# The last half's rows brought in and normalised one half earlier, its neighbour's scalings on GpSimd, and the exactness check moved from half 11 to half 1

## The chip, the cores and the metric

The kernel runs on one core of a Trainium2 chip. The metric is the device time of one execution in microseconds (us). Three runs of the kernel before took 2614.74, 2616.55 and 2617.44 us; the median is 2616.55 us.

## The reference: what is computed

`x` has 3327 rows of 512 numbers, `adj` is a 3327 x 3327 matrix of zeros and ones (about 1% ones).

```python
def gat_layer(x, W, adj):                 # used twice, W of 512 x 1024
    Wh, Ws = split(x @ W, 2, axis=-1)
    a = softmax(Wh @ Ws.T, axis=-1) * adj
    return leaky_relu(a @ Wh + x, 0.01)

def sign_layer(x, adj, weight):           # weight of 512 x 512
    xw = maximum(sign(x), 0) @ sign(weight).T
    return relu(adj @ xw)

x = layernorm(x + gat_layer(gat_layer(x, W[0], adj), W[1], adj))
x = layernorm(x + sign_layer(x, adj, weight))
```

The change concerns the very last part: `adj @ xw`, the relu, the sum with the layer-normed rows, and the last layernorm.

## The kernel before, in words

The 3327 rows are 26 tiles of 128 (the last has 127), two tiles make a half, so there are NQ = 13 halves, numbered 0 to 12. Two attention passes take most of the time: each goes through 13 x 13 steps of a half of output rows against a half of keys, with seven products instead of eight for each 2 x 2 block of tiles. The second pass also leaves behind what the last layer needs: `h_d` in DRAM holds the rows `h` ahead of the first layernorm, `mv` their means and variances, `adj_d` the seven block sums of the adjacency in 8 bits, and `xw` the product of signs in 16 bits. It also counts, in `cnt`, the adjacency entries that are neither 0 nor 1 (`exact`): 8 bits carry the block sums only of such a matrix.

`finale` is the last layer. For each half g it has 91 matmuls (`aggregate`, L1138): 13 pairs of tiles by seven products, which collect in four PSUM banks, b = 0 to 3. (In half 12 two of the products have other places and one a bank of its own.) Many matmuls of halves 0 and 1 are issued earlier, as filling between the last steps of attention; what half 1 has left are 14. Around the matmuls of a half, these are the steps:

- `load_h(g + 1)`: SyncE loads two tiles of `h_d` into `ho` (four buffers in all, so a tile waits until the tile four before it has been stored).
- `standard(t)` (L1166, L1167): two ScalarE instructions give a tile of `ho` the first layernorm.
- `take_out(g, b)` (L1179 to L1190): ScalarE copies the first product of bank 0 (L1179), VectorE adds the products together into `c`.
- `moments(t)` (L1195 to L1201): VectorE computes `ho = max(c, 0) + ho` (L1195) and its mean and variance (L1197, L1199), ScalarE the square root (L1201).
- `scaled(t)` (L1208, L1209): VectorE takes the reciprocal and scales the tile; then GpSimd issues the store to `out` (L115).
- `check`, once: VectorE reduces `cnt` to one number per partition (`bad`, L1213), TensorE transposes that (`pbad`, L1215), VectorE reduces it to one number and casts it (`flag`, `flag_i`, L1216, L1217).

After half 12's matmuls every engine loads `flag_i` into a register and branches (L1260, L1261). If the count is zero, the short tail is run: half 12 is taken out of PSUM piece by piece, each piece followed by its share of the moments (L1274, L1275, L1280), the second tile is scaled on ScalarE (L1303, L1304), the first on VectorE (L1209), and both are stored. Otherwise the layer is computed again from the adjacency in 32 bits.

No scheduler orders this work. Each half collects pairs of a place between 0 and 1 and a function in the list `work`; the matmuls stand at even distances, the other steps at the places written beside them. The list is sorted by place and run in that order, and each engine gets its instructions in the order in which they are written. An engine runs its own list strictly in order: if an instruction waits, all behind it wait.

Of the kernel before, what the change touches and what calls it, by code (L numbers as in the profile page):

```python
# [15 lines left out]
ALU = mybir.AluOpType  # L16
AX = mybir.AxisListType
# [13 lines left out]
def kernel(  # L31
# [8 lines left out]
    nc = tc.nc  # L40
# [6 lines left out]
    NQ = NT // 2  # L47
    assert NT % 2 == 0 and D == 4 * P

    def rows(t):  # L50
        return min(P, N - t * P)
# [7 lines left out]
    def half_tiles(g):  # L59

        return (2 * g, 2 * g + 1)
# [28 lines left out]
    cnt = keep.tile([P, NQ * NQ], F32, name="cnt")  # L90
# [19 lines left out]
    def load_rows(eng, dst, src, r):  # L110

        cut = r - r % 16
        engines = eng if isinstance(eng, tuple) else (eng,)
        if cut:
            engines[0].dma_start(out=dst[:cut], in_=src[:cut])  # L115
        if cut < r:
            engines[-1].dma_start(out=dst[cut:r], in_=src[cut:r])
# [437 lines left out]
    def attention(l, att):  # L555
# [514 lines left out]
        for e in fill:  # L1070
            aggregate(*e)
        finale(att)


# [42 lines left out]
    def load_aggregate(g, s):  # L1117
        n = min(JL, NQ - s * JL)
        t = slot([P, JL, 7, P], F8, f"ahl_{g}_{s}")
        nc.sync.dma_start(out=t[:, :n], in_=adj_d[g][:, s * JL : s * JL + n])  # L1120
        for p in range(n):
            ah[g, s * JL + p] = t[:, p]

    def aggregate(g, b, p, i):
        if p == 0 and (i == BANKS[b][0] or (g, i) == (NQ - 1, 5)):
            pool, tag = (ps_acc, "acc") if g % 2 else (ps_ch, "ch") if b < 3 else (ps_tr, "tr")
            if g == NQ - 1 and i == 5:

                (pool, tag), b = (ps_acc, "acc"), 4
            po[g, b] = pool.tile([P, 2, HD], F32, tag=tag, name=f"agg_{g}_{b}")  # L1130
        x1, x2, t = xw[2 * p], xw[2 * p + 1], xt.get(p)
        if i < 2:
            of = (x1, x2)[i][:, :HD]
        else:
            of = (t[:, 1], t[:, 2], t[:, 0], x2[:, HD:], t[:, 3])[i - 2]

        own = (g, i) == (NQ - 1, 5)
        nc.tensor.matmul(  # L1138
            po[g, 4 if own else b][:, i % 2], ah[g, p][:, BLOCKS[i]], of,
            start=(p == 0 and (own or i % 2 == 0)), stop=(p == NQ - 1), skip_group_check=True,  # L1140
        )

    def finale(att):
# [5 lines left out]
        bad = small.tile([P, 1], F32, tag="bad", bufs=1, name="bad")  # L1149
# [8 lines left out]
        def load_h(g):  # L1158
            for t in half_tiles(g):
                h = h_of[t] = att.tile([P, D], F32, tag="adj", bufs=4, name=f"ho_{t}")  # L1160
                load_rows(nc.sync, h, h_d[t * P : t * P + rows(t), :], rows(t))

        def standard(t):
            h = h_of[t][: rows(t)]
            r = rows(t)
            nc.scalar.activation(h, h, AF.Identity, bias=nmean[:r, t : t + 1])  # L1166
            nc.scalar.activation(h, h, AF.Identity, scale=rstd[:r, t : t + 1])  # L1167

        def take_out(g, b):
            def s(name):  # L1170
                tmp[name] = att.tile([P, HD], F32, tag=f"o{name}", bufs=1, name=f"a{name}_{g}")
                return tmp[name]

            if b == 0:
                c_of[g] = [ring.tile([P, D], F32, tag="h", name=f"c_{t}") for t in half_tiles(g)]
            lo, hi = c_of[g]
            k = po[g, b]
            if b == 0:
                nc.scalar.copy(s("p1"), k[:, 0])  # L1179
                nc.vector.tensor_tensor(lo[:, :HD], k[:, 1], tmp["p1"], ALU.add)  # L1180
            elif b == 1:
                nc.vector.tensor_tensor(s("u2"), k[:, 0], tmp["p1"], ALU.add)
                nc.vector.tensor_tensor(s("u3"), k[:, 1], tmp["u2"], ALU.add)
            elif b == 2:
                c12 = lo[:, HD:]
                nc.vector.tensor_tensor(c12, k[:, 0], tmp["u2"], ALU.add)
                nc.vector.tensor_tensor(c12, k[:, 1], c12, ALU.add)
                nc.vector.tensor_tensor(hi[:, HD:], k[:, 0], tmp["u3"], ALU.add)
            else:
                nc.vector.tensor_tensor(hi[:, :HD], k[:, 0], tmp["u3"], ALU.add)  # L1190

        def moments(t, c, tag=""):
            r = rows(t)
            h = h_of[t][:r]
            nc.vector.scalar_tensor_tensor(h, c[:r], 0.0, h, ALU.max, ALU.add)  # L1195
            st = small.tile([P, 6], F32, tag="bn", name=f"bo{tag}_{t}")
            nc.vector.bn_stats(st[:r], h)  # L1197
            m2 = small.tile([P, 2], F32, tag="mv2", name=f"mo{tag}_{t}")
            nc.vector.bn_aggr(m2[:r], st[:r])  # L1199
            rs = small.tile([P, 1], F32, tag="rs", name=f"rs{tag}_{t}")  # L1200
            nc.scalar.activation(rs[:r], m2[:r, 1:2], AF.Sqrt, bias=eps[:r])  # L1201
            out_of[t] = m2, rs

        def scaled(t, *engines):
            r = rows(t)
            h = h_of[t][:r]
            m2, rs = out_of[t]
            nc.vector.reciprocal(rs[:r], rs[:r])  # L1208
            nc.vector.tensor_scalar(h, h, m2[:r, 0:1], rs[:r], ALU.subtract, ALU.mult)  # L1209
            load_rows(engines, out[t * P : t * P + r, :], h, r)  # L1210

        def check():
            nc.vector.reduce_max(bad, cnt, axis=AX.X)  # L1213
            pb = ps_tr.tile([1, P], F32, tag="tr", name="pbad")
            nc.tensor.transpose(pb, bad, ident)  # L1215
            nc.vector.reduce_max(flag, pb, axis=AX.X)  # L1216
            nc.vector.tensor_copy(flag_i, flag)  # L1217
# [4 lines left out]
        for g in range(NQ):  # L1222
            todo = [
                (b, p, i) for b in range(4) for p in range(NQ) for i in BANKS[b]
                if g > 1 or (g, b) == (0, 3) or p >= EARLY
            ]
            if g == NQ - 1:

                todo = [e for e in todo if e[0] < 2] + [
                    (b, p, i) for b, i in ((3, 6), (2, 4), (2, 5)) for p in range(NQ)  # L1230
                ]
            work = [
                ((n + 0.5) / len(todo), lambda e=e: aggregate(g, *e))
                for n, e in enumerate(todo)
            ]
            done = {b: (n + 1) / len(todo) for n, (b, p, i) in enumerate(todo)}
            t1, t2 = half_tiles(g)
            if g + 3 < NQ:
                work += [
                    (s / NS, lambda s=s: load_aggregate(g + 3, s)) for s in range(NS)  # L1240
                ]
            if g + 1 < NQ:
                work.append((0.5, lambda: load_h(g + 1)))
            work += [(0.1, lambda: standard(t1)), (0.4, lambda: standard(t2))]
            if g == NQ - 2:
                work.append((0.95, check))
            if g < NQ - 1:
                for b in range(3):
                    work.append((done[b] + 0.02, lambda b=b: take_out(g, b)))
                work += [(0.98, lambda: moments(t1, c_of[g][0]))]  # L1250
            if g > 0:
                u1, u2 = half_tiles(g - 1)
                work += [
                    (0.05, lambda: take_out(g - 1, 3)), (0.08, lambda: scaled(u1, nc.gpsimd)),
                    (0.1, lambda: moments(u2, c_of[g - 1][1])),
                    (0.2, lambda: scaled(u2, nc.gpsimd)),
                ]
            for _, do in sorted(work, key=lambda e: e[0]):
                do()
        inexact = nc.values_load(flag_i[0:1, 0:1], min_val=0, max_val=2 * CW)  # L1260
        with tc.If(inexact < 1) as cmp:  # L1261

            t1, t2 = half_tiles(g0)
# [33 lines left out]
            r = rows(t2)  # L1297
            m2, rs = out_of[t2]
# [3 lines left out]
            h = h_of[t2][:r]  # L1302
# [4 lines left out]
            half(t1, hi)  # L1307
            both(t1)
            scaled(t1, nc.sync)
        with cmp.Else():  # L1310

            for t in range(NT):
                r = rows(t)
# [13 lines left out]
                h = h_of[t] = att.tile([P, D], F32, tag="adj", bufs=4, name=f"hf_{t}")  # L1327
# [44 lines left out]
```

## Time and profile before

The profiled execution took 2613.8 us, of which the span that the profile shows is 2612.0 us; the table gives places in that span. The profiled run is 2.75 us shorter than the median of the three timed runs.

| stage | us from the span's start | what stands there |
|---|---|---|
| filling matmuls, 16-bit, and the rest of half 0 and 1 | 2472 to 2491.8 | TensorE back to back |
| half 2 | 2491.84 to 2501.77 | 91 matmuls, 9.93 us; VectorE busy 9.17 us |
| half 10 | 2571.31 to 2581.24 | 91 matmuls, 9.93 us; VectorE busy 6.95 us |
| half 11 | 2581.24 to 2592.1 | 91 matmuls and the check |
| half 12's matmuls | 2592.1 to 2602.2 | the last work of TensorE |
| tail on VectorE and ScalarE | 2598.08 to 2606.76 | taking out, moments, scaling |
| last stores | 2605.56 to 2612.0 | |

In half 12 TensorE and VectorE work beside each other. GpSimd issues nothing but stores in this part of the kernel. TensorE is busy 99% of the span, VectorE 81%, GpSimd 42%, ScalarE 31%. Rows of the timeline give the start and the duration of an instruction or a merged group; in brackets stands how long its engine had been idle, and for whom it waited.

### The profile page before, as it was taken

Reading aid. Unit: us, or ns where it says so; the run is one execution under the profiler, and the core shown is the slowest. Engines: PE = TensorE matmul, PEld = TensorE weight load, DVE = VectorE, ACT = ScalarE, POOL = GpSimd, SP = SyncE. Lnnn points to the kernel's source line nnn. Section 1 sums busy time; section 2 is a strip of 40 time slices with the busy share of each in tenths; the row PEclk is TensorE's granted clock in tenths of the full one; section 3 lists DMA queues with packets and bytes.
Section 4 is the critical chain, followed back from the end, with each engine's and each line's share of the span. In section 5 each row is a group of like instructions: output and inputs, shape, how many; then the busy total and the mean of one; then the engine's idle time right before and its main releaser. Section 6 shows DMA issues by size and latency. Waiting matters only on the chain. (4 is left out here: it accounts for less than half of the span.)

```text
span 2612.0 us, 40098 instructions
## 1 busy us (share of the span) xinstructions
PE 2581.2 (99%) x12536; PEld 2235.2 (86%) x12536; DVE 2111.2 (81%) x4422; ACT 800.5 (31%) x1978; POOL 1095.4 (42%) x2026
## 2 busy tenths in 40 slices
PE   9999999999999999999999999999999999999998
PEld 7888888888888888887888888888888888888787
DVE  5754888899888996768874689989899898776976
ACT  3323332333333332221332333333333333222143
POOL 3640344444434444456662044434444444454611
PEclk9999999999999999999999999999999999999999
DMA  6855777777777877698865668777787777677775
GB/s 210 295 195 176 244 240 265 241 267 253 256 247 238 277 237 237 224 264 251 301 242 178 227 223 282 246 254 257 239 282 245 249 261 237 232 260 260 261 254 184
DMA packets 309784, 639.15 MB, mean 245 GB/s; under 512 B 35049, under 2 KB 177987, under 8 KB 308028
## 3 DMA queue, kind: packets, MB, share of 16 engines
q1 hardware_dynamic: 273868, 530.29, 62.4%
q0 software_dynamic: 35696, 106.21, 10.9%
q8 instruction: 103, 1.69, 0.3%
q14 instruction: 117, 0.96, 0.1%
HBM read 529.69 MB, written 106.67 MB: 244 GB/s over the span
## 5 line engine op out<-in xcount | busy, mean ns | idle before, releaser
L586 PE MATMUL pZ<-gs,xs 128*128 128x256 f32 x2496 | 636.9, 380 | 3.0 <-ACT u L603 2.9
L793 POOL TENSOR_TENSOR as<-s 128x128 f32<-128x128 f32 x338 | 163.2, 483 | 1051.2 <-DVE s L755 866.5
L586 PEld LDWEIGHTS pZ<-gs,xs 128*128 128x128 f32 x2496 | 473.0, 190 | 71.3 <-ACT u L603 6.4
L820 PE MATMUL acc<-ws,s 128*128 128x256 f32 x1352 | 402.4, 379 | 0.5 <-DVE h L855 0.5
L820 PE MATMUL acc<-wh,s 128*128 128x256 f32 x1352 | 355.7, 379 | 0.7 <-DVE s L755 0.4
L820 PE MATMUL acc<-ws,as 128*128 128x256 f32 x1352 | 348.0, 380 | 4.2 <-POOL as L795 4.1
L745 ACT ACTIVATE s<-s 128x512 f32<-128x512 f32 x338 | 213.3, 631 | 396.6 <-DVE s L739 395.6
L586 PE MATMUL pY<-gs,xs 128*128 128x256 f32 x1248 | 320.9, 380 | 4.4 <-ACT p L603 4.4
L820 PEld LDWEIGHTS acc<-ws,as 128*128 128x128 f32 x1352 | 256.0, 190 | 45.8 <-POOL as L795 8.6
L820 PEld LDWEIGHTS acc<-wh,s 128*128 128x128 f32 x1352 | 256.6, 190 | 36.7 <-DVE s L755 1.9
L820 PEld LDWEIGHTS acc<-ws,s 128*128 128x128 f32 x1352 | 255.7, 190 | 36.0 <-DVE h L855 1.7
L586 PEld LDWEIGHTS pY<-gs,xs 128*128 128x128 f32 x1248 | 236.5, 190 | 38.7 <-ACT p L603 6.7
L656 DVE TENSOR_TENSOR top<-top,s 128x512 f32<-128x512 f32 x286 | 200.7, 716 | 72.3 <-ACT s L643 52.8
L739 DVE TENSOR_TENSOR s<-s,off 128x512 f32<-128x512 f32 x338 | 246.4, 729 | 0.6
L755 DVE TENSOR_TENSOR s<-s,adj 128x512 f32<-128x512 f32 x338 | 239.1, 707 | 9.5 <-DMA adj<-in_adjT_dram 1.5
L750 DVE TENSOR_TENSOR total<-total,s 128x512 f32<-128x512 f32 x312 | 230.4, 738 | 0.0
L795 POOL TENSOR_TENSOR as<-s 128x128 f32<-128x128 f32 x338 | 202.6, 599 | 26.5
L603 ACT COPY u<-pZ 128x256 f32<-128x256 f32 x312 | 115.6, 371 | 306.9 <-PE pZ L586 303.8
L820 PE MATMUL acc<-wh,as 128*128 128x256 f32 x676 | 202.4, 381 | 0.0
L794 POOL TENSOR_TENSOR s<-s 128x128 f32<-128x128 f32 x338 | 184.4, 546 | 27.4
L796 POOL TENSOR_TENSOR as<-s,as 128x128 f32<-128x128 f32 x338 | 182.2, 539 | 26.5
L628 DVE TENSOR_TENSOR s<-p,u 128x256 f32<-128x256 f32 x156 | 67.0, 430 | 137.8 <-ACT u L603 136.7
(219 smaller groups left out, 3890.8 us busy)
## 6 DMA issues: line engine op xcount, KB each, us to landing
ws<-ws_d SPq DMA_DIRECT2D x338, 512.0 KB, 3.8
xs<-xs_d SPq DMA_DIRECT2D x182, 512.0 KB, 5.7
adj<-in_adjT_dram SPq DMA_DIRECT2D x324, 256.0 KB, 4.2
xs<-xs_d SPq DMA_DIRECT2D x156, 384.0 KB, 6.2
gs_d<-gsp POOLq DMA_DIRECT2D x88, 256.0 KB, 3.0
gs<-gs_d SPq DMA_DIRECT2D x12, 1792.0 KB, 11.1
adj_d<-ab POOLq DMA_DIRECT2D x169, 112.0 KB, 3.9
ahl<-adj_d SPq DMA_DIRECT2D x78, 224.0 KB, 4.7
```

What stands on the lines that cost most here:

```text
L586: nc.tensor.matmul(ch[bank], xs[c, q, a][:, k], gs[c][:, b, k], start=(start and k == 0), stop=(k == 1), skip_group_check=True,)
L603: nc.scalar.copy(ch[name], ch[bank])
L656: nc.vector.tensor_tensor(top[i], top[i], t, ALU.max)
L739: nc.vector.tensor_tensor(s, s, off[g].to_broadcast([P, 2, HW]), ALU.subtract)
L745: nc.scalar.activation(sc[g, q], sc[g, q], AF.Exp)
L750: nc.vector.tensor_tensor(total[g], total[g], sc[g, q], ALU.add)
L755: nc.vector.tensor_tensor(s, s, adj[g, q], ALU.mult)
L793: nc.gpsimd.tensor_tensor(s3, a11, a21, ALU.subtract)
L794: nc.gpsimd.tensor_tensor(a21, a21, a22, ALU.add)
L795: nc.gpsimd.tensor_tensor(s2, a21, a11, ALU.subtract)
L796: nc.gpsimd.tensor_tensor(s4, a12, s2, ALU.subtract)
L820: nc.tensor.matmul(acc[g][i // 2][:, i % 2], a[i], b[i], start=(q == 0 and i % 2 == 0), stop=(q == NQ - 1), skip_group_check=True,)
```

## The change

Four things are moved. First, the check: the reduction of `cnt` stands at place 0.5 of half 1, the rest of the check at place 0.8 of half 1, instead of all at place 0.95 of half 11. Second, the loads of half 12's two tiles stand at place 0.3 of half 11 instead of 0.5. Third, `standard` of these two tiles stands at place 0.9 of half 11, instead of 0.1 and 0.4 of half 12. Fourth, `scaled` of half 11's two tiles (it stands in half 12) runs its scaling on GpSimd instead of VectorE; the reciprocal stays on VectorE. In the order of the built programs TensorE has `pbad` between the third and the fourth of bank 2's four matmuls of half 1, so with three matmuls of half 1 behind it. VectorE has `bad` behind `take_out(1, 0)`, which stands behind both scalings of half 0. ScalarE has the four instructions of half 12's `standard` ahead of the square root of half 11's first tile.

```diff
-        def scaled(t, *engines):
+        def scaled(t, *engines, on=nc.vector):
             r = rows(t)
             h = h_of[t][:r]
             m2, rs = out_of[t]
             nc.vector.reciprocal(rs[:r], rs[:r])
-            nc.vector.tensor_scalar(h, h, m2[:r, 0:1], rs[:r], ALU.subtract, ALU.mult)
+            on.tensor_scalar(h, h, m2[:r, 0:1], rs[:r], ALU.subtract, ALU.mult)
             load_rows(engines, out[t * P : t * P + r, :], h, r)
 
         def check():
-            nc.vector.reduce_max(bad, cnt, axis=AX.X)
             pb = ps_tr.tile([1, P], F32, tag="tr", name="pbad")
             nc.tensor.transpose(pb, bad, ident)
             nc.vector.reduce_max(flag, pb, axis=AX.X)
...
             if g + 1 < NQ:
-                work.append((0.5, lambda: load_h(g + 1)))
-            work += [(0.1, lambda: standard(t1)), (0.4, lambda: standard(t2))]
+                work.append((0.5 if g < NQ - 2 else 0.3, lambda: load_h(g + 1)))
+            if g < NQ - 1:
+                work += [(0.1, lambda: standard(t1)), (0.4, lambda: standard(t2))]
             if g == NQ - 2:
-                work.append((0.95, check))
+
+                work += [(0.9, lambda t=t: standard(t)) for t in half_tiles(g + 1)]
+            if g == 1:
+                work += [
+                    (0.5, lambda: nc.vector.reduce_max(bad, cnt, axis=AX.X)), (0.8, check)
+                ]
...
             if g > 0:
                 u1, u2 = half_tiles(g - 1)
+                on = nc.gpsimd if g == NQ - 1 else nc.vector
                 work += [
-                    (0.05, lambda: take_out(g - 1, 3)), (0.08, lambda: scaled(u1, nc.gpsimd)),
+                    (0.05, lambda: take_out(g - 1, 3)),
+                    (0.08, lambda: scaled(u1, nc.gpsimd, on=on)),
                     (0.1, lambda: moments(u2, c_of[g - 1][1])),
-                    (0.2, lambda: scaled(u2, nc.gpsimd)),
+                    (0.2, lambda: scaled(u2, nc.gpsimd, on=on)),
                 ]
```

## The prediction

> **What bounds the kernel now.** I read the totals per engine first, then the chain of waits that ended last, then the timeline around the two places where the check stands before and after, then the granted clock. TensorE is at its limit and the chain says where: 943 matmuls of the last layer without a break, up to half 11's end. Only after that does the chain leave TensorE.
>
> ```profile
> PE 2581.2 (99%) x12536; PEld 2235.2 (86%) x12536; DVE 2111.2 (81%) x4422; ACT 800.5 (31%) x1978; POOL 1095.4 (42%) x2026
> ```
>
> ```profile
> 2486.82 103.11 PE agg L1138 x943
> ...
> 2591.17 0.25 DVE bad L1213
> ...
> 2591.46 0.28 PE pbad L1215
> ...
> 2593.80 0.30 ACT rs L1201
> ...
> 2594.33 0.55 DVE ho L1209
> ...
> 2596.66 0.71 ACT ho L1166
> ...
> 2597.39 0.47 ACT ho L1167
> ...
> 2598.08 0.38 ACT ap L1179
> ...
> 2598.55 0.44 DVE c L1180
> ...
> 2604.06 0.44 DVE c L1306
> ```
>
> So whatever delays TensorE between 2486.82 and 2589.93 delays the end by as much, and what is saved behind 2591 is saved on a chain of VectorE and ScalarE instructions. The tile's own view confirms that the check costs TensorE little where it stands, because VectorE is up to date there:
>
> ```profile
> L1213 DVE TENSOR_REDUCE bad<-cnt x1: 319/319/319, 2591.1 to 2591.1; 128x1 f32<-128x169 f32 x1
> ...
>   PE pbad L1215: 0.7, 1
> ```
>
> Eleven halves earlier VectorE is not up to date. Two answers of the timeline, TensorE's rows and VectorE's:
>
> ```profile
> 2491.46 0.38 PE L1138 MATMUL agg<-wh,ahl 128*128 128x256 f16 x2
> 2491.84 0.60 PE L1138 MATMUL agg<-xw,ahl 128*128 128x256 f16 x4
> ```
>
> ```profile
> 2498.45 0.55 DVE L1209 TENSOR_SCALAR ho<-ho,mo,rs 128x512 f32<-128x512 f32 x1
> 2498.92 0.42 DVE L1180 TENSOR_TENSOR c<-agg,ap 128x256 f32<-128x256 f32 x1
> 2499.25 0.41 DVE L1182 TENSOR_TENSOR au<-agg,ap 128x256 f32<-128x256 f32 x1
> ```
>
> TensorE starts half 2 at 2491.84. VectorE does take_out(1, 0), behind which `bad` is written in the new order, at 2498.92. TensorE is about 8 us ahead, because half 1 has only 14 matmuls left (1.5 us) while VectorE has all of half 0's and half 1's steps to do.
>
> **Part 1, the check into half 1: the wait.** In TensorE's new order three matmuls of half 1 stand behind `pbad`. One takes 9.93 / 91 = 0.109 us, so TensorE comes to `pbad` at 2491.84 - 3 x 0.109 = 2491.5. VectorE comes to `bad` at 2499.25, the start that L1182 has now; nothing ahead of it is changed. From the start of `bad` to that of `pbad` the old place shows 2591.09 to 2591.46, 0.37 us. So `pbad` starts at 2499.62, the next matmul 0.11 later (2591.46 to 2591.57 in the old place), three matmuls take 0.33, and half 2 starts at 2500.06 instead of 2491.84: **+8.2 us**. Behind the waiting instruction stand 1004 matmuls, without a listed wait up to `pbad`'s old place; they need 9.93 us per half, VectorE 6.95 in half 10, so VectorE catches up and TensorE does not. No later slack takes the delay in. For VectorE the check is 0.3 + 0.3 + 0.1 us more in half 1, where it then waits for TensorE anyway: nothing.
>
> **Part 2, the clock after that wait.** TensorE has never paused for 8 us in the trace before. The rows that bear on it are its first matmuls and its end:
>
> ```profile
> 3.69 1.95 PE L347 MATMUL pxt<-ident,xr 128*128 128x128 f32 x8 [3.69 <-DMA xr<-in_x_dram]
> ...
> 8.32 2.07 PE L407 MATMUL pZ_wh<-wa,xT 128*128 128x256 f32 x4
> 10.18 0.64 PE L260 MATMUL pwT<-ident,wa 128*128 128x128 f32 x4
> 10.66 1.03 PE L407 MATMUL pX_wh<-wa,xT 128*128 128x256 f32 x4
> ```
>
> ```profile
> 2603.50:2604.00 0.50, 0.00 (x0) 0.00 (x0) 0.48 (x4) 0.30 (x1) 0.00 (x0) 1.00 0.12 33
> 2604.00:2604.50 0.50, 0.00 (x0) 0.00 (x0) 0.49 (x2) 0.44 (x1) 0.00 (x0) 0.88 0.00 0
> 2604.50:2605.00 0.50, 0.00 (x0) 0.00 (x0) 0.44 (x2) 0.47 (x2) 0.00 (x0) 0.50 0.00 0
> ```
>
> In the windows the granted clock stands behind the five engines' busy times: it falls to 0.50 at about 2604.4, some 2.2 us after the last matmul's end (2602.21). A wait of 8 us is longer, so I expect half clock after it. How long: the same four matmuls take 1.86 us at 8.32 and 0.87 at 10.66, so half speed lasted until about 10.2 (the windows give no fall of the clock there, so I go by the durations). Counted from the last wait (8.32) that is 1.9 us of dense work, from the wait before (5.94) 4.2, from the first matmul 6.5. Half the stretch is lost: 0.9, 2.1 or 3.2 us. Ends are 0 (the clock stays) and 3.3; a gain is excluded, as nothing is granted above 1.00. I take **+2.1**, the middle reading, since the new work is dense from its start, as it was from 5.94 but for 0.15 us.
> The Trainium skill, "TensorE: Matmul & The Clock Gate", section on the HAM clock gate, states that an idle window of about 3.4 us halves the clock and about 3.4 us of sustained work restores it. By that the loss would be an estimated 1.7 us and the whole sum 0.4 less; the fall after only 2.2 us at the end of this trace fits a window that runs freely.
>
> **Part 3, half 12's loads and normal form in half 11.** Places in this part are those of before; in the new run all stand later by parts 1 and 2. The loads stand at 0.3 instead of 0.5, but they wait for a buffer: the store of half 10's second tile is issued by GpSimd at 2586.84, and SyncE issues the last piece of the load (15 rows) at 2589.96 now. Scaling and store of half 10 are unchanged, so the load isn't sooner. SyncE has nothing behind it in that stage. Loads of `ho` land 2.3 to 4.2 us after issue, this piece at 2592.3 at the earliest; the two instructions on ScalarE (0.72 + 0.75) end at 2593.7, and only then comes the square root of half 11's first tile, which the new order puts behind them. It starts at 2593.80 now, behind the check (VectorE 2591.17 to 2592.22, 1.05 us). So the 1.05 us that the check leaves free there is taken by the wait for the load: **0**, from -1.0 (load very early) to +1.8 (it lands after 4.2).
>
> **Part 4, the scalings on GpSimd, and ScalarE free in half 12.** VectorE loses 0.54 us at 2594.33 (to 2594.87), so the second tile's moments and square root come 0.54 sooner: 2595.91 instead of 2596.45. Behind this square root ScalarE has no `standard` any more, so the copy L1179 comes after the branch (2597.92 to 2598.08 now, some 0.2 us): about 2596.3 instead of 2598.08. VectorE, without its second scaling, has its reciprocal done at 2596.4 and passes its branch: L1180 starts at about 2596.7 instead of 2598.55, -1.85. The chain from L1180 is unchanged to the end, if TensorE is in time. Half 12's matmuls start 0.94 sooner in these places (2591.17 instead of 2592.11, the check being gone). The product that L1292 reads is complete when the last group of 13 begins, 2600.63 now, so 2599.7 then, and 0.16 later for the pipeline; L1292, at 2602.05 now, could be 2.2 sooner at most. So the gain is under 2.2.
> The price on GpSimd: the trace has no scaling on it. Bounds are VectorE's own 0.55 and the 1.71 of a two-input 128x512 operation on GpSimd (L207). Even with 1.71 and 0.54 for each store, both are issued by 2598.8; GpSimd's next duty, the 15 rows, comes at 2605.83 - 1.85 = 2604. The cover is 5 us. Beside it VectorE reads two tiles from SBUF in L1195 and L1274: L739 beside GpSimd takes 0.65 to 0.95 us, so up to 0.3 each. I take 0.15 in all: **-1.7**, from -2.2 to -1.2.
> The Trainium skill, "SBUF — State Buffer", section on who interferes with whom, says that a VectorE instruction with two SBUF inputs contends with a GpSimd instruction that reads SBUF, the one that issues first holding the ports for its whole length. Had each of the two waited a whole 1.71, the estimate would be 3.4 more; the 338 two-input L755 beside GpSimd's work have a median of 0.691, against 0.68 of L1195 with GpSimd silent, so I do not use it.
>
> **Sum.** 8.2 + 2.1 + 0 - 1.7 = +8.6 on the profiled 2613.8: 2622.4. The median of the runs is 2.75 above the profiled run, so in its terms 2616.55 + 8.6, say **2625**.
>
> **Rivals.** (a) *TensorE does not wait.* If the reduction reaches TensorE in time, only part 4 is left: 2616.55 - 1.7 = 2614.9, no slower. For it speaks that the old place cost 0.7 us alone; against it the 8 us between the rows above. It decides from the point where VectorE is less than 1.7 us late. (b) *The wait is there, the clock stays:* 2616.55 + 6.5 = 2623. For it: every full slice of the page shows 9 tenths or more. Against: the fall at 2604.4. (c) *The tail gets worse:* the load lands late (+1.8) or GpSimd and VectorE hold each other up (two waits of 1.71): 2627 to 2628.5. For it: L739's 0.95; against: the medians.
>
> **Numbers.** Forecast (slower by 6.2 to 10.5 us) 0.76; (b) 0.10; (c) 0.07; (a) 0.06; something unseen that gains, 0.01. A run of this kernel differs from the median by up to 1.8 us; a difference under about 0.2%, 5.2 us, cannot be told from none. Slower by more: 0.76 + 0.07 + most of (b) = 0.92. Within: (a) and the rest of (b), 0.06; faster 0.02. Low end: 2616.55 + 8.2 + 0 - 2.2 = 2622.5, less 1.3 for the runs; high end: 2616.55 + 8.2 + 3.3 - 1.2 + 1.3 = 2628.2.
>
> **What would show it.** `pbad` near 2499.6 with an idle time of some 8 us ahead of it, waiting for `bad`; windows behind it with a granted clock of 0.5 for 2 to 6 us; half 2's 91 matmuls in 11 to 13 us; no wait of TensorE for a check in half 11; the root of half 11's first tile on ScalarE directly behind half 12's second tile; GpSimd rows of L1209 between 0.6 and 1.7. The forecast is wrong if VectorE is nearer to TensorE in half 1 than the trace says, or if the tail gives back more than 2.2.

## The result, and the profile after

The changed kernel takes 2626.42 us in the median of seven runs (2623.29 to 2627.37), the kernel before on the same chip 2616.14 us (2613.61 to 2617.44). The ratio is 1.0036 with a 95% interval of 1.0027 to 1.0046: the change costs 7 to 12 us. The forecast was 2625 us.

The profiled execution took 2626.94 us, its span is 2625.2. The first rows to read are those of the tile `bad` and, from the timeline, of `pbad` and what follows it on TensorE:

```profile
L1250 DVE TENSOR_REDUCE bad<-cnt x1: 319/319/319, 2503.7 to 2503.7; 128x1 f32<-128x169 f32 x1
...
  PE pbad L1214: 8.1, 1
```

```profile
2504.07 0.37 PE L1214 MATMUL pbad<-ident,bad 128*1 128x128 f32 x1 [8.11 <-DVE bad L1250]
2504.24 0.42 PE L1138 MATMUL agg<-xw,ahl 128*128 128x256 f16 x1
2504.45 0.64 PE L1138 MATMUL agg<-wh,ahl 128*128 128x256 f16 x2
2504.88 4.19 PE L1138 MATMUL agg<-xw,ahl 128*128 128x256 f16 x26
```

TensorE waits 8.11 us for `bad`, where it had waited 0.7. Behind the wait a matmul starts 0.21 us after the one before it, where 0.11 was usual. Stages of half a microsecond (the granted clock stands behind the five engines' busy times) show why:

```profile
2500.00:2500.50 0.50, 0.00 (x0) 0.00 (x0) 0.41 (x2) 0.50 (x2) 0.00 (x0) 0.97 0.00 0
2500.50:2501.00 0.50, 0.00 (x0) 0.00 (x0) 0.50 (x2) 0.47 (x2) 0.00 (x0) 0.50 0.00 0
...
2507.00:2507.50 0.50, 0.50 (x6) 0.40 (x4) 0.50 (x1) 0.00 (x0) 0.00 (x0) 0.70 0.12 49
2507.50:2508.00 0.50, 0.50 (x7) 0.46 (x5) 0.47 (x3) 0.13 (x1) 0.00 (x0) 1.00 1.01 393
```

The clock falls at 2500.47, while TensorE waits, and rises at 2507.3. The 3.2 us of work in between, from 2504.07, lose half, 1.6 us.

The chain of waits no longer names TensorE: followed back from the end it goes over the stores of GpSimd, with 70% of the window asked for under "issue". So only its part for the tail is used. Shown here is what led to half 11's square root and what followed it:

```profile
2598.42 4.21 DMA out_dram<-ho
2602.68 2.73 DMA ho<-h_d
...
2605.50 0.73 ACT ho L1166
...
2606.88 0.71 ACT ho L1166
...
2608.34 0.19 ACT rs L1201
...
2611.00 0.38 ACT ap L1179
...
2611.47 0.44 DVE c L1180
...
2616.98 0.43 DVE c L1313
```

Half 12's first tile could be loaded only when the store of half 10's first tile had landed (4.21 us), and landed itself at 2605.41. Then come four ScalarE instructions for the two tiles, and only then the square root (L1201) that half 11's first tile waits for.

The part ahead of the last layer differs from run to run: the product of signs of the last tile (L921), with which I begin the last layer, starts at 2485.74 in the profiled run of before and at 2490.18 in that of after; nothing is changed ahead of it, and in the ten profiled runs of this case it lies anywhere between 2483.1 and 2490.2. (In four of them, the changed kernel's among these, the clock is low for 3.4 us near 460 us too; see the last section.) So all that follows is measured from that instruction. Each column is a difference of starts in the timeline, or of a start and the end of the span; L1186 is the take-out of half 11's third bank, the place where VectorE waits for TensorE for the last time before the tail, and "last L1209" the scaling of the last tile.

| kernel | L921 to L1186 | L1186 to L1180 of half 12 | L1186 to last L1209 | L1186 to end of span | whole |
|---|---|---|---|---|---|
| before | 104.22 | 8.59 | 16.25 | 22.04 | 126.26 |
| after | 114.01 | 7.28 | 14.95 | 21.01 | 135.02 |
| e1: reduction early | 110.09 | 7.24 | 14.90 | 20.70 | 130.79 |
| e2: check alone | 114.44 | 7.54 | 15.21 | 21.09 | 135.53 |
| e3: check in half 6 | 109.23 | 7.62 | 15.28 | 21.18 | 130.41 |
| e4: check in half 10 | 105.15 | 7.09 | 14.75 | 20.83 | 125.98 |
| f1: whole check first | 104.30 | 7.04 | 14.69 | 20.60 | 124.90 |
| f2: f1, normal form split | 104.29 | 6.03 | 14.11 | 19.87 | 124.16 |
| f3: f1, old normal form | 104.30 | 6.96 | 14.63 | 20.69 | 124.99 |
| f4: f1, no GpSimd | 104.30 | 8.00 | 15.66 | 21.40 | 125.70 |

Before to after: +9.79 up to L1186 (8.2 for the wait, 1.6 for the clock), -1.03 behind it, together +8.76. The medians say 10.28; their interval takes in both.

### The profile page after: what moved, and what is told of

Its sections match the earlier page's. It is cut to its first block, busy times and chain, and to the rows that moved or that the text cites. A ratio compares the mean times of both kernels' runs of the same rounds, so it can differ in the third digit from the quotient of the medians.

```text
span 2625.2 us, 40079 instructions
## 1 busy us (share of the span) xinstructions
PE 2583.9 (98%) x12511; PEld 2237.5 (85%) x12536; DVE 2112.3 (80%) x4420; ACT 800.5 (30%) x1978; POOL 1100.5 (42%) x2028
```

## Experiments

Two theories stood against each other. The first: the loss is the wait of TensorE for VectorE in half 1, and the clock behind it. The second: it lies in the tail, in GpSimd's scalings or in ScalarE's new order. e1 to e4 ran on one chip, on which before took 2614.36 us (29 runs); f1 to f4 on one with 2615.65 us (23 runs).

### e2: the check alone

```diff
# against the kernel before
-            nc.vector.reduce_max(bad, cnt, axis=AX.X)
             pb = ps_tr.tile([1, P], F32, tag="tr", name="pbad")
...
-            if g == NQ - 2:
-                work.append((0.95, check))
+            if g == 1:
+                work += [
+                    (0.5, lambda: nc.vector.reduce_max(bad, cnt, axis=AX.X)), (0.8, check)
+                ]
```

> The kernel before with the move of the check alone (reduction at 0.5 and the rest at 0.8 of half 1); loads, normal form and scalings as before. Theory: the wait of 8.1 us and 1.6 us of half clock are all here, less about 1.0 us that VectorE saves behind half 11 because the check is gone there: 8.5 to 9 us above the kernel before, as slow as the changed kernel to within 0.5 us. Rival (the tail costs part of it): at least 2 us faster than the changed kernel.

Measured: 2622.22 us, ratio 1.0029 (1.0018 to 1.0040). `pbad` waits 8.1 us for `bad`; up to L1186 the last layer takes 10.22 us more than before, behind it 0.95 less, +9.27 in all against +8.76 in the changed kernel, 0.5 apart as the theory had it. The clock was low for 4.1 us of work here (2500.86 to 2504.97) against 3.2, which explains 0.45 of that. So the move of the check has the whole loss. And it has nearly the whole gain of the tail: 21.09 against 21.01. The three other edits of the change together bring 0.08 us to the end of the span (0.26 to the last L1209).

### e1: the reduction early, the transpose still in half 1

```diff
# against the changed kernel
         product_sums(NQ - 1)
+        nc.vector.reduce_max(bad, cnt, axis=AX.X)
         constants()
...
             if g == 1:
-                work += [
-                    (0.5, lambda: nc.vector.reduce_max(bad, cnt, axis=AX.X)), (0.8, check)
-                ]
+                work.append((0.8, check))
```

> The changed kernel with one edit: the reduction of cnt to bad stands directly ahead of the constants of the last layer, where VectorE has time, instead of at place 0.5 of half 1; the transpose on TensorE stays in half 1. Theory (the place of bad in VectorE's order makes TensorE wait 8.1 us and halves its clock for 3.2 us): no wait of pbad above 0.2 us, granted clock 1.00 up to the end, 8.2 + 1.6 us less than the changed kernel, so 2616.5 us, between 0 and 2 us under the kernel before. Rival (the loss lies in the tail, in GpSimd's scalings or ScalarE's order): no less than 2623 us.

Measured: 2619.16 us, ratio 1.0020 (1.0010 to 1.0029). Both were wrong: 4 us of the loss went, 4 us stayed. The timeline's row of the transpose:

```profile
2496.57 0.27 PE L1214 MATMUL pbad<-ident,bad 128*1 128x128 f32 x1 [4.09 <-DVE c L1190]
```

It waits no more for `bad`, but for L1190. That is `take_out(0, 3)`, which empties the PSUM bank in which half 0's fourth product lies; `pbad` is put into the same bank, the only one of its pool. I had not looked for this second wait, because the first one covered it. VectorE's steps of half 0 delay it too. The clock then did something that I had not expected either:

```profile
2496.50:2497.00 0.50, 0.43 (x4) 0.39 (x5) 0.41 (x3) 0.50 (x2) 0.00 (x0) 1.00 0.00 0
2497.00:2497.50 0.50, 0.50 (x5) 0.37 (x3) 0.50 (x2) 0.47 (x2) 0.00 (x0) 0.53 0.00 0
2500.00:2500.50 0.50, 0.50 (x4) 0.38 (x3) 0.50 (x2) 0.47 (x2) 0.00 (x0) 0.55 0.00 0
2500.50:2501.00 0.50, 0.50 (x7) 0.44 (x6) 0.47 (x2) 0.33 (x1) 0.00 (x0) 1.00 0.05 12
```

It falls at 2497.03, half a microsecond after TensorE is back at work, and rises at 2500.45: 3.42 us at half clock, all of them work, 1.7 us lost. 4.1 + 0.1 for `pbad` + 1.7 = 5.9 us, the difference in the table (110.09 - 104.22).

### e3: the check in half 6

```diff
# against the changed kernel
-            if g == 1:
+            if g == 6:
```

> The changed kernel with the check in half 6 instead of half 1. By the trace of before VectorE is about 2.3 us behind TensorE there, so pbad waits 2.3 to 3 us. Theory of a clock that falls only after an idle time of about 2 us or more: a short fall or none, loss 2.5 to 4 us in all in place of 9.8, so 1.5 to 3 us above the kernel before. Rival (the clock's loss is fixed at 1.6 us for every wait): 4.3 us and more of loss.

Measured: 2618.66 us, ratio 1.0015 (1.0006 to 1.0025); the last layer is 4.15 us longer than before, its part up to L1186 5.01 us. My theory of the clock fell. The wait is 3.42 us, a little over the 3 expected, and the clock falls for 3.4 us here too:

```profile
2543.00:2543.50 0.50, 0.00 (x0) 0.00 (x0) 0.46 (x2) 0.14 (x1) 0.00 (x0) 1.00 0.83 315
2543.50:2544.00 0.50, 0.00 (x0) 0.00 (x0) 0.50 (x3) 0.00 (x0) 0.05 (x1) 0.59 1.07 430
2546.50:2547.00 0.50, 0.50 (x4) 0.32 (x3) 0.50 (x3) 0.00 (x0) 0.00 (x0) 0.50 1.00 363
2547.00:2547.50 0.50, 0.50 (x6) 0.45 (x5) 0.50 (x1) 0.00 (x0) 0.00 (x0) 1.00 1.08 426
```

From about 2543.6 to 2547.0, of which 2.7 us are work: 1.35 us lost, beside 3.4 + 0.1. The rival, a loss that hardly depends on the length of the wait, is right over the four waits seen: 1.35 at 3.4 us, 1.7 at 4.1, 1.6 and 2.05 at 8.1. What it does depend on, as the two waits of 8.1 us show, stands in the last section.

### e4: the check in half 10

```diff
# against the changed kernel
-            if g == 1:
+            if g == 10:
```

> The changed kernel with the check in half 10, where VectorE is ahead of TensorE. Theory: no wait of TensorE, the tail as in the changed kernel, so 1 us under the kernel before, the same as with the early reduction in half 1 to within 0.3 us. Rival (it is the half in which the transpose stands, not VectorE's lag): a wait of TensorE of several us here also.

Measured: 2611.86 us, ratio 0.9995 (0.9985 to 1.0004). TensorE waits 0.3 us for `bad` and 0.2 us for `flag` (half 10's fourth product wants the bank), the clock stays at 1.00. With `pbad` itself and the restarts this comes to 0.93 us up to L1186 (105.15 against 104.22), so a small loss is left here. So it is VectorE's lag that counts, not the distance from the end. The comparison with e1 that I had expected came to nothing, because e1 was no kernel without a wait.

### f1: the whole check ahead of half 0

```diff
# against the changed kernel
+        nc.vector.reduce_max(bad, cnt, axis=AX.X)
         product_sums(NQ - 1)
+        check()
         constants()
...
-            if g == 1:
-                work += [
-                    (0.5, lambda: nc.vector.reduce_max(bad, cnt, axis=AX.X)), (0.8, check)
-                ]
```

Here VectorE has idle time for the reduction (4.47 us in the trace before, ahead of the last product sums), and the bank is free: half 0's fourth product takes it later.

> The changed kernel with the whole check at the start of the last layer: the reduction of cnt ahead of the last product sums, transpose and flag behind them, before half 0's fourth product takes the PSUM bank that the transpose uses too. Theory (in half 1 the transpose stands behind two things that VectorE does late, the reduction and the emptying of that bank; each alone costs a wait of 4 us or more and up to 1.7 us of half clock): no wait of TensorE above 0.2 us, granted clock 1.00, last layer 126.3 - 1.2 = 125.1 us from the last product of signs to the end of the span, 1 us under the kernel before. Rival (any place in the first halves costs TensorE several us): 4 us and more above the kernel before.

Measured: 2612.54 us, ratio 0.9986 (0.9978 to 0.9995), faster than before. The row of `pbad` has no idle time ahead of it, the clock is 1.00, and the last layer takes 124.90 us, 1.36 less than before (expected 1.2).

```profile
2488.31 0.27 PE L1214 MATMUL pbad<-ident,bad 128*1 128x128 f32 x1
```

That takes 10.1 us from the last layer of the changed kernel by the place of the check alone.

### f2, f3, f4: what the three other edits are worth

f1 makes them readable. f2 moves the normal form of half 12's second tile behind the square root of half 11's first:

```diff
# against f1
             if g == NQ - 2:
-                work += [(0.9, lambda t=t: standard(t)) for t in half_tiles(g + 1)]
+                work.append((0.9, lambda: standard(half_tiles(g + 1)[0])))
...
                 on = nc.gpsimd if g == NQ - 1 else nc.vector
+                if g == NQ - 1:
+                    work.append((0.07, lambda: standard(t2)))
```

> As f1, and half 12's second tile gets its normal form behind the square root of half 11's first tile instead of ahead of it. Theory (in the changed kernel that root waits for the late load and four ScalarE instructions, 1.1 us): from the take-out of half 11's third bank (L1186) to L1180 of half 12 some 6.1 us instead of 7.28, to the last scaling about 14.0 instead of 14.95 since TensorE's products limit it then; 2 us under the kernel before. Rival (the root is not what the tail waits for): 14.9 as in f1.

f3 takes the early normal form back (the loads stay at 0.3):

```diff
# against f1
-            if g < NQ - 1:
-                work += [(0.1, lambda: standard(t1)), (0.4, lambda: standard(t2))]
-            if g == NQ - 2:
-                work += [(0.9, lambda t=t: standard(t)) for t in half_tiles(g + 1)]
+            work += [(0.1, lambda: standard(t1)), (0.4, lambda: standard(t2))]
```

> As f1, but half 12's normal form at its old places in half 12; only the scalings on GpSimd are left of the changes to the tail. Theory (moving the normal form ahead costs as much as the check's leaving gives): 7.0 us from L1186 to L1180 and 14.7 to the last scaling, 0.2 to 0.3 less than in the changed kernel. Rival (the early normal form is what shortens the tail): over 7.5 and 15.2.

f4 takes GpSimd's scalings back:

```diff
# against f1
-                on = nc.gpsimd if g == NQ - 1 else nc.vector
+                on = nc.vector
```

> As f1, but both scalings stay on VectorE; only the early loads and normal form are left of the changes to the tail. Theory (GpSimd's scalings take 2.1 to 2.5 us but save VectorE 0.54 twice): 7.8 us from L1186 to L1180, 15.4 to the last scaling. Rival (GpSimd's work holds VectorE up as much as it takes from it): 7.3 and 14.95 as in the changed kernel.

Measured, from L1186 to the last L1209: f1 14.69, f2 14.11, f3 14.63, f4 15.66, and single times of 2614.56 us (f3) and 2612.58 us (f4). All are within 0.3 of what the theory gave. But f3 and f4 have one run each, and the five kernels with the changed kernel's tail (after, e1, e3, e4 and f1) differ among themselves, 14.69 to 15.28, because the loads of half 12 land sooner or later. So f1, the lowest of them, is no sure measure. The early normal form with GpSimd's scalings is worth nothing: f3 (14.63) is below all five. GpSimd's scalings are worth between 0.4 and 1.0 beside the early normal form (f4 against the five), and 0.58 without it (f3 against e2, 15.21; neither waits for the loads there). Without them the early normal form costs 0.45 (f4 against e2, one profile each). So the worth of one edit depends on the others. With a wait fewer, the early normal form is worth 0.5 after all (f2 against f3): f2 has the lowest median of the kernels here, 2610.85 us, ratio 0.9985 (0.9976 to 0.9994; f1's interval is nearly the same), and 2.1 us less than before in the last layer. ScalarE in f1 and in f2, from the timeline; the rows in f1 are those that the square root has to wait for:

```profile
2593.23 0.72 ACT L1166 ACTIVATE ho<-ho,nmean 127x512 f32<-127x512 f32 x1 [0.20 <-DMA ho<-h_d]
2593.99 0.72 ACT L1167 ACTIVATE ho<-ho,rstd 127x512 f32<-127x512 f32 x1
2594.62 0.28 ACT L1201 ACTIVATE rs<-mo,eps 128x1 f32<-128x1 f32 x1
```

```profile
2592.12 0.29 ACT L1201 ACTIVATE rs<-mo,eps 128x1 f32<-128x1 f32 x1 [0.27 <-DVE mo L1199]
2592.33 0.71 ACT L1166 ACTIVATE ho<-ho,nmean 127x512 f32<-127x512 f32 x1
2593.07 0.72 ACT L1167 ACTIVATE ho<-ho,rstd 127x512 f32<-127x512 f32 x1
```

In f2 the root waits for its own moments alone. L1180 then starts 1.01 us sooner than in f1, but the last scaling only 0.58: VectorE now waits 0.36 us for TensorE in the tail, as the expectation had it (it put 14.0 for 14.11).

## Why the prediction was right, point by point

**Part 1, the wait.** Right to a tenth: `pbad` was put at 2499.62; in the run it starts at 2504.07, which is 2499.63 after taking off the 4.44 us by which this run's last layer begins later. All 8.2 us reach the end, because TensorE stays back to back up to half 12 and has no slack. What the working left out is the bank: had the reduction been in time, 4.1 us of wait and 1.7 of clock would have been left (e1). Rival (a), "TensorE does not wait", needed two conditions, not the one that the text gave.

**Part 2, the clock.** Right that it falls, a size too high: 2.1 forecast, 1.6 measured, 2.05 in e2. The reading of the start of the trace, 4.2 us, was the wrong measure. The low stretch lasted 3.42 us in e1 and 6.8, twice as long, in the changed kernel and in e2; only the part with work in it costs. The estimate from the Trainium skill ("TensorE: Matmul & The Clock Gate", the section on the HAM clock gate), 1.7 us by windows of 3.4 us that run freely, was the better one. The low stretches of 3.4 and 6.8 us agree with windows of that length, and so does the fall in e1, half a microsecond after the work had begun again. The page's condition of an idle window is not what the traces show: in the window at whose end the clock fell in e1, TensorE was busy for 0.46 us (last section).

**Part 3, loads and normal form: 0.** Nearly right, for a slightly other reason. The text took the load of the second tile as the one that ends last. In the run the first tile's load was late (the store of half 10's first tile, for whose buffer it waits, took 4.21 us to land), and the second tile's instructions queued behind the first's on ScalarE. The square root started at 2608.25, 14.45 us later than before, and all of half 11 is 14.23 later (L1186, 2604.19 against 2589.96): +0.2 us instead of 0. So the 1.05 us that the check's leaving freed were eaten there, as forecast, and 0.2 besides. f2, in which the root starts 2.79 us behind L1186 instead of 4.06 (before, with the check, 3.84), shows that they were to be had.

**Part 4, GpSimd and the branch: -1.7.** This term was wrong in size, twice. First the saving: from L1186 to L1180 it is 1.31 us; adding the 0.2 of part 3, part 4 gave 1.5, not 1.7. ScalarE's load of the flag and its branch had been hidden behind the second `standard` before (0.2 us were seen); now they stand open, and the copy L1179 starts 0.69 us after the square root's start, where the working had 0.4. The 0.15 us allowed for GpSimd and VectorE in each other's way were not needed. The chain's rows:

```profile
2610.31 0.29 ACT rs L1201
2610.61 0.18 ACTq L1267
2610.78 0.06 issue
2610.84 0.05 ACTq L1268
...
2611.00 0.38 ACT ap L1179
```

(The timeline puts ScalarE's idle time here down to VectorE's reciprocal; that ended at 2610.80, ahead of L1268.) Second the price on GpSimd, bounded at 1.71, is 2.46 and 2.09:

```profile
2608.83 2.46 POOL L1209 TENSOR_SCALAR ho<-ho,mo,rs 128x512 f32<-128x512 f32 x1 [7.22 <-DVE rs L1208]
2612.25 2.09 POOL L1209 TENSOR_SCALAR ho<-ho,mo,rs 128x512 f32<-128x512 f32 x1
```

The cover that was named holds: the second store is issued at 2614.63, the 15 rows at 2618.76. VectorE's L1195, begun 0.19 us ahead of the first scaling, takes 0.69 us, against 0.68 with GpSimd silent, but there VectorE came first. f3 has the other order: L1275, which reads two tiles in SBUF, begins 0.62 us behind GpSimd's second scaling and lies wholly under it. It takes 0.44 us, against 0.43 in e2, where GpSimd is silent.

```profile
2598.81 2.09 POOL L1209 TENSOR_SCALAR ho<-ho,mo,rs 128x512 f32<-128x512 f32 x1
2599.43 0.44 DVE L1275 SCALAR_TENSOR_TENSOR ho<-c,ho 128x256 f32<-128x256 f32 x1
```

So the contention that the Trainium skill states in "SBUF — State Buffer" (section on who interferes with whom) did not show on VectorE's side. Whether GpSimd's 2.46 has a share of it was not tried; no run here has its scaling with VectorE silent.

**The sum.** +8.6 was forecast on the profiled execution, +8.76 is measured from L921 to the end. The errors of part 2 (-0.5), part 3 (+0.2), part 4 (+0.2) and the last store (from the last L1209 to the end of the span 6.06 us instead of 5.79, +0.27) nearly cancel, so the total speaks for part 1 and not for the others; that it is right to 0.2 us is luck. Rival (b), at +6.5, lay inside the range of 6.2 to 10.5 that the forecast gave itself (its own terms add up to 6.0 and 10.3, ahead of the 1.3 for the runs), so the time alone could not have decided against (b). The granted clock excludes (b), and the table (c).

## What to carry to other kernels

Moving a step to an earlier place is free only where the engine that feeds it has got there too: an engine that runs ahead has its lead exactly where others are behind, so compare the times at which each engine reaches the new place, not the places. Look for all that the moved instruction needs, the buffer that it writes as well as the operand that it reads; the longer of two waits hides the other. A wait of a few microseconds on TensorE can cost more than itself, here 1.4 to 2.1 us more.

## What was not expected of the hardware

The granted clock fell to one half after waits of 3.4 us (e3) and 4.1 us (e1) as it did after 8.1, in e1 only when the work had begun again, and stayed there for 3.4 us or twice that. The clock records of the ten traces show what decides. Within a trace all changes of the clock lie whole multiples of 3.41 us apart; in the changed kernel they come 132, 133, 729, 731 and 764 such windows after the first rise at 12.16 us. Of the some 7600 windows at full clock in the ten traces, 18 have TensorE busy for 1.39 us or less, and the clock fell at the end of each of them; it fell at the end of no other, and the emptiest of these had 1.43. Four of them (the first number behind the length is TensorE's busy time): from e1 and from e2 one with a fall at its end, from e2 and from the kernel before one without.

```profile
2493.62:2497.03 3.41, 0.46 (x5) 0.41 (x6) 3.22 (x9) 0.84 (x3) 0.00 (x0) 1.00 0.00 0
456.98:460.39 3.41, 1.39 (x8) 0.88 (x6) 0.99 (x5) 1.00 (x4) 2.19 (x5) 1.00 0.89 331
2491.32:2494.73 3.41, 1.43 (x14) 1.03 (x11) 2.07 (x6) 2.55 (x5) 0.00 (x0) 1.00 0.14 47
457.39:460.81 3.42, 1.66 (x8) 1.15 (x7) 1.32 (x5) 1.15 (x4) 1.78 (x4) 1.00 0.86 319
```

So the loss depends on where the wait lies in these windows, which differs from run to run: the pauses near 460 us, where the program is the same in every kernel, lowered the clock in four of the ten traces. In all of them the clock rose again at the end of the first window with 2.73 us of work or more, and after the one with 0.71 it stayed low (e2); so the wait of 8.1 us cost 1.6 us once and 2.05 the other time.

GpSimd took 2.1 to 2.5 us for the scaling of a 128x512 tile in 32 bits with two numbers per partition, for which VectorE takes 0.55.
